# Audio tower on one core: another order of the token tiles, DCT tiles in three and two, and moved sums in the first gate

## The chip, the core and the metric

The kernel runs on one core of a Trainium2 chip. The metric is the device time of one execution in microseconds (us). A core has five engines that run their own instruction streams: TensorE (PE; PEld is its weight load), VectorE (DVE), ScalarE (ACT), GpSimd (POOL) and SyncE (SP), which here only issues transfers. Sixteen DMA engines move data between HBM and the core's memory. Matrix results land in PSUM.

## The reference, cut to what matters

The input is 64 rows of 80000 samples. Each row is cut into 157 frames of 512 samples; a frame is a token.

```
h = frames @ D.T                                   # orthonormal DCT of 512
y = layernorm(h)
key, query phases = tanh(y @ Wk), tanh(y @ Wq)     # 4 sets of 8 planes
V = y @ Wv
total = sum over sets of  weight * Re(cumsum(e^(i key) V) * conj(e^(i query)))
total = gate * total + (1 - gate) * positional part of the same form
h = h + y + (total / sqrt(8 * position)) @ Wo      # gate = sigmoid(y @ Wg)
z = layernorm(h)
expert = argmax(softmax(mean over tokens of z @ Wg2))     # 1 of 16, for each row
h = h + score * (z @ We[expert] + be[expert])
```

The cumulative sums are computed as causal attention: a matrix of scores between query and key tokens, masked so that a query sees keys up to its own position, and then a product with V.

## The kernel before, in words

**Groups and tiles.** Four rows of the input make a group (`GB` = 4), so there are 16 groups. The 157 tokens of a row are padded to 160 and cut into five blocks of 32 (`Q`). A token tile `n` holds block `n` of all four rows: 128 tokens. Tile 4 is `TAIL`. Within the transposed buffers (`xT`, `gT`) the tiles lie in the order of `SLOT`: slots 0 to 4 hold tiles 0, 1, TAIL, 2, 3.

**Scores.** `scores` (L596) multiplies, for each tile of 32 keys, the keys' phasors with those of a range of query slots, `SEES[n]`. A range has to be one stretch of slots that covers every query which may see the block. With tiles in order of position, tile 2 needs blocks 2, 3 and 4, and tile 3 needs 3 and 4; since TAIL lies in slot 2, both take slots 2 to 4. The widths are 160, 128, 96, 96 and 32 queries, `NS` = 512 in all. Where a range is wider than the causal one, `hmask` holds zeros. VectorE makes `att` from the scores: two versions of 512 columns (L597, L598).

**Read.** `read` (L611) works on one of four chunks of 128 features at a time. For each tile `n` and each of the four rows it multiplies the 32 keys' values (32 rows of the array, 128 columns of weights) with both versions of `att` in the tile's range. The four rows take four row groups of the array and run side by side, into four banks in two PSUM tiles. The first matmul of a bank has the start flag, so it has to cover all 320 columns. VectorE then multiplies the banks with the gate and adds (L619), four operations for each chunk.

**PSUM.** One pool of four tiles of two banks serves all stages, in rotation. An allocation waits until the tile four allocations back has been read for the last time.

**Order.** The order of the instructions is written out by hand. Each engine takes its instructions in that order, so a function that is called earlier stands earlier in all the queues that it uses. A period for group `g` is `project_and_values`, `gate`, `experts_and_embedding`, `attention`. In `experts_and_embedding` TensorE computes the five expert tiles of group `g - 1` (`expert`, L814, four column groups side by side) and the DCT of the five tiles of group `g + 1` (`embed`, L250 and L252, the whole array). `embed_statistics` is a ScalarE copy, four VectorE operations and four small POOL operations (L226 to L229, L265); `embed_res` is one ScalarE operation (L279), the last reader of the DCT tile's PSUM. `add_bv` adds a bias to two value tiles on POOL, `add_bias` and `expert_out` are VectorE operations on an expert tile, and `expert_out` issues its output transfers.

**Group 0** has no experts before it. `first_gate` interleaves its four gate parts (L558) with the DCT of group 1, with `weigh` (a VectorE scaling of the query phasors that the scores need), with `fold_twice(1, 1)` (four VectorE operations that prepare group 1's frames), with `add_bo` (a POOL addition) and with `weights`, which makes sums of weight quarters on VectorE, two of eight at a call.

**The end.** After the last group's attention the experts of group 14 run, five tiles in the order `ORDER` (TAIL, 0, 1, 2, 3). Within the second of them the last group's rows are routed, and `fetch` gathers its experts' weights with indirect transfers that POOL issues (L768), in two halves, with the expert bias (L798) between. The last group's experts follow: all tiles for the first half of the features, then tile by tile for the second. Outputs are issued by SP (L830), in the last group half of them by ScalarE.

Of the kernel before, what the change touches and what calls it, by code (L numbers as in the profile page):

```python
# [22 lines left out]
P = 128  # L23
# [9 lines left out]
HT = P // 2  # L33
HN = HT + 2 * P
LT = L - Q * TAIL
SETS, PLANES = 4, 8
F = SETS * PLANES
E = 16
# [2 lines left out]
ROUND = 1.5 * 2.0**23  # L41


SEES = [(0, LP), (Q, LP), (2 * Q, LP), (2 * Q, LP), (2 * Q, 3 * Q)]
START = [sum(hi - lo for lo, hi in SEES[:n]) for n in range(NM)]
NS = sum(hi - lo for lo, hi in SEES)

# [4 lines left out]
def audio_tower(ctx: ExitStack, tc: tile.TileContext, a, out):  # L52
# [69 lines left out]
    def fold_twice(g, m):  # L122

        if g < NG:
            ft, even = half(S[g]["xT"], m), S[g].pop(("even", m))
            add(ft[:, 2], even[:, 0], even[:, 1])
            sub(ft[:, 3], even[:, 0], even[:, 1])
            for n in range(2):
                to, by = ft[:, n], ft[:, 1 - n]
                nc.vector.scalar_tensor_tensor(to, by, lift[:, n : n + 1], to, ALU.mult, ALU.add)  # L130
# [416 lines left out]
    def weigh():  # L547
        nc.vector.tensor_scalar(qf[: 2 * F], qf[: 2 * F], wvec, None, ALU.mult)

    def gate_part(g, o):  # L550

        s = S[g]
        if o == 0:
            s["gT"] = p1.tile([P, C, 2 * HN], F32, tag="gT", name="gT")
        ps = psum()
        for k in range(2):
            for c in range(C):
                nc.tensor.matmul(  # L558
                    ps[:, k, :HN],
                    wg[:, c, o * P : (o + 1) * P],  # L560
                    half(s["xT"], k)[:, c],
                    start=(c == 0),
                    stop=(c == C - 1),
                )
        to = s["gT"][:, o].rearrange("p (m t) -> p m t", m=2)
        nc.scalar.activation(to, by_halves(ps), AF.Tanh, bias=hbg[:, o : o + 1], scale=0.5)
# [33 lines left out]
    def read(g, c):  # L600

        s = S[g]
        parts = [psum(), psum()]
        banks = [ps[:, b, : 2 * LP] for ps in parts for b in range(2)]
        for n in range(NM):
            for i in range(GB):
                q = slice(Q * i, Q * (i + 1))
                lo, hi = SEES[n]
                to = banks[i].rearrange("p (s t) -> p s t", s=2)[:, :, lo:hi]
                by = att[q, :, START[n] : START[n] + hi - lo]  # L610
                nc.tensor.matmul(  # L611
                    to, s["v", n][q, c * P : (c + 1) * P], by, start=(n == 0), stop=(n == TAIL)
                )
        for k, ps in enumerate(parts):
            of = slice(2 * k, 2 * k + 2)
            r = ps[:, :, : 2 * LP].rearrange("p b (s n t) -> p b s n t", s=2, n=NM)
            th = s["gT"][:, c].rearrange("p (n b t) -> p b n t", n=NM, b=GB)[:, of]
            for n, op in enumerate((ALU.mult, ALU.add)):
                nc.vector.tensor_tensor(th, r[:, :, n], th, op)  # L619
# [201 lines left out]

    def expert_out(g, n, ps):
        s = S[g]
        o = s["res"][n]
        nc.vector.scalar_tensor_tensor(o, ps, s["gate"], o, ALU.mult, ALU.add)  # L825
        for i in range(GB):

            for lo, hi in ((0, Q),) if n < TAIL else ((0, Q // 2), (Q // 2, LT)):
                queue = nc.sync if g + 1 < NG or i % 2 == 0 else nc.scalar
                queue.dma_start(out=out[GB * g + i, Q * n + lo : Q * n + hi, :], in_=o[Q * i + lo : Q * i + hi, :])  # L830

    def expert(g, n, between=lambda c: None):
        ps = psum()
# [84 lines left out]
    def first_gate():  # L918

        made = chain(weight_sums(wv, t_v), weight_sums(wo, t_o))  # L920

        def weights():
            next(made)
            next(made)

        gate_part(0, 0)
        embed(1, 1)
        embed_statistics(1, 1)
        weigh()
        embed_res(1, 1)  # L930
        fold_twice(1, 1)
        add_bo(0, 0)
        weights()
        gate_part(0, 1)
        scores(0)
        embed(1, 2)
        embed_statistics(1, 2)
        embed_res(1, 2)
        add_bo(0, 1)
        weights()  # L940
        gate_part(0, 2)
        for n in (3, TAIL):
            embed(1, n)
            embed_statistics(1, n)
        for n in (3, TAIL):
            embed_res(1, n)
        add_bo(0, 2)
        weights()
        gate_part(0, 3)
        for n in (3, TAIL):  # L950
            add_bo(0, n)
        weights()
        load_half(2, 0)
        load_half(2, 1)

# [61 lines left out]
    def experts_and_embedding(g):  # L1017

        new = g + 1

        def embedded(n):
            embed_statistics(new, n)
            embed_res(new, n)

        add_bias(g - 1, TAIL)
        expert(g - 1, TAIL)
        embed(new, 0)
        embed(new, 1)
        embed_statistics(new, 0)
        embed_statistics(new, 1)  # L1030
        add_bias(g - 1, 0)
        embed_res(new, 0)
        embed_res(new, 1)
        add_bv(g, 0)
        load_half(g + 2, 0)
        load_half(g + 2, 1)
        expert(g - 1, 0)
        embed(new, 2)
        embed_statistics(new, 2)
        embed_res(new, 2)  # L1040
        add_bias(g - 1, 1)
        add_bv(g, 1)
        expert(g - 1, 1)
        embed(new, 3)
        embed(new, TAIL)
        embed_statistics(new, 3)
        embed_statistics(new, TAIL)
        embed_res(new, 3)
        embed_res(new, TAIL)
        add_bias(g - 1, 2)  # L1050
        expert(g - 1, 2)
        add_bias(g - 1, 3)
        expert(g - 1, 3)
# [98 lines left out]
def _constants():  # L1152
    k = np.arange(D)[:, None].astype(np.float64)
    t = np.arange(D)[None, :].astype(np.float64)
    dct = np.cos(np.pi * (2.0 * t + 1.0) * k / (2.0 * D))
    scale = np.full((D, 1), np.sqrt(2.0 / D))
    scale[0, 0] = np.sqrt(1.0 / D)
    dct = (scale * dct).astype(np.float32)
    ahead = slice(0, P)

    angle = np.pi * (2.0 * np.arange(P)[:, None] + 1.0) / (2.0 * D)
    j = np.arange(P + 1)[None, :]
    cosines = np.sqrt(2.0 / D) * np.cos(angle) * np.where(j < P, np.cos(4 * j * angle), 0.0)
    sines = np.sqrt(2.0 / D) / np.cos(angle) * np.sin(4 * j * angle)

    tables = [cosines[:, :P].T, cosines[:, 1:].T, sines[:, :P].T, -sines[:, 1:].T, dct[0::4, ahead], dct[2::4, ahead]]

    def trig(half, n, turn):

        rows = np.array([[-1.0, -turn, PI / 2]] * half + [[1.0, turn, 0.0]] * half)  # L1170
        return np.tile(rows, (n, 1)).astype(np.float32)


    at = np.concatenate([np.arange(Q * n, Q * (n + 1)) for n in np.argsort(SLOT)])
    norm = 1.0 / np.sqrt(np.float64(PLANES) * (at + 1))
    causal = (np.arange(LP)[:, None] <= at[None, :]) * norm[None, :] * (at < L)[None, :]
    causal[L:] = 0.0
    masks = [causal[Q * n : Q * (n + 1), lo:hi] for n, (lo, hi) in enumerate(SEES)]
    setsel = np.tile(np.repeat(np.eye(SETS), PLANES, axis=0), (2, 1))
    f = lambda x: np.ascontiguousarray(x, dtype=np.float32)  # L1180

    sums = [x.sum(axis=0) for x in tables]
    table_sums = np.concatenate([sums[0] + sums[1], sums[2] + sums[3], sums[4], sums[5]]) / -D
    return {
        "dct_e": f(np.stack([dct[0::4, ahead].T, dct[2::4, ahead].T], axis=1)),
        "trig_o": f(np.stack([cosines, sines], axis=1)),
        "tables": f(np.stack(tables, axis=1)),
        "table_sums": f(table_sums),
        "lift": f(np.concatenate([np.tan(angle), -np.sin(angle) * np.cos(angle)], axis=1)),
        "ptrig": trig(PLANES, 1, 2 * PI),  # L1190
        "pos": f(np.tile(at, (2 * PLANES, 1))),
        "hmask": f(0.5 * np.tile(np.concatenate(masks, axis=1), (GB, 1))),
        "setsel": f(setsel),
        "revexp": f(np.tile(E - np.arange(E), (P, GB, 1))),
        "rowbase": f(np.stack([n * (np.arange(P) + P * E) + k for n, k in ((1, 0), (2, 0), (2, 1))], axis=1)),
    }
# [12 lines left out]
def _frames(x):  # L1209

    x = np.pad(x, [(0, 0), (0, LP * D - T_IN)]).reshape(NG, GB, NM, Q, C, P)
    x = np.stack([x[..., 0, :], x[..., 1, ::-1], x[..., 3, ::-1], x[..., 2, :]], axis=4)
    x = x[:, :, np.argsort(SLOT)].transpose(0, 5, 4, 2, 1, 3).reshape(NG, P, C, 2, HN)
    return np.ascontiguousarray(x.transpose(0, 3, 1, 2, 4))


# [34 lines left out]
```

## Time and profile before

| | |
|---|---|
| time, median of 3 | 1396.61 us (1396.16 to 1398.22) |
| profiled execution | 1396.78 us, span 1395.0 us |
| TensorE busy | 1383.8 us, 99% of the span |
| VectorE busy | 1033.5 us, 74% |
| GpSimd busy | 598.8 us, 43% |
| ScalarE busy | 399.7 us, 29% |
| moved by DMA | 119.72 MB, 86 GB/s on average |

The costliest lines on TensorE are the experts (L814, 270.3 us of busy time in the steady groups), the value and output products (L370), the gate products (L577) and the read (L611, 127.8 us). In the profile one fp32 matmul stands as two records, so that a tile of 16 expert matmuls is 32 records. Records of one tile on different row or column groups overlap, and a busy sum counts overlapping time once. The number behind `<-` in a waits line is the total in us, then how often, then the longest.

### The profile page before, as it was taken

Reading aid. Unit: us, or ns where it says so; the run is one execution under the profiler, and the core shown is the slowest. Engines: PE = TensorE matmul, PEld = TensorE weight load, DVE = VectorE, ACT = ScalarE, POOL = GpSimd, SP = SyncE. Lnnn points to the kernel's source line nnn. Section 1 sums busy time; section 2 is a strip of 40 time slices with the busy share of each in tenths; the row PEclk is TensorE's granted clock in tenths of the full one; section 3 lists DMA queues with packets and bytes.
Section 4 is the critical chain, followed back from the end, with each engine's and each line's share of the span. In section 5 each row is a group of like instructions: output and inputs, shape, how many; then the busy total and the mean of one; then the engine's idle time right before and its main releaser. Section 6 shows DMA issues by size and latency. Waiting matters only on the chain.

```text
span 1395.0 us, 26923 instructions
## 1 busy us (share of the span) xinstructions
PE 1383.8 (99%) x10656; PEld 919.3 (66%) x10656; DVE 1033.5 (74%) x2076; ACT 399.7 (29%) x690; POOL 598.8 (43%) x846
## 2 busy tenths in 40 slices
PE   9999999999999999999999999999999999999998
PEld 6677575766758667575675757667585675757762
DVE  5778686877868677786776868778686777867673
ACT  2414242231423314242141422314232142421410
POOL 2463544425543354534535444255533545345312
PEclk9999999999999999999999999999999999999999
DMA  7013204032230413205032140322304132040305
GB/s 223 1 39 128 76 28 162 16 130 75 86 116 3 153 53 129 76 1 184 21 129 76 40 152 14 133 73 106 97 2 147 59 128 76 1 151 16 129 8 195
DMA packets 47484, 119.72 MB, mean 86 GB/s; under 512 B 9264, under 2 KB 26176, under 8 KB 39424
## 3 DMA queue, kind: packets, MB, share of 16 engines
q0 software_dynamic: 11072, 71.31, 13.1%
q1 hardware_dynamic: 35788, 46.06, 11.3%
q8 instruction: 84, 1.38, 0.4%
q10 hardware_dynamic: 500, 0.64, 0.2%
q14 instruction: 40, 0.33, 0.1%
HBM read 97.41 MB, written 20.58 MB: 85 GB/s over the span
## 4 chain that ended last, share of the span: by engine, by line
PE 96%; DMA 1%; ACT 1%; DVE 1%; POOL 1%; issue 0%; SPq 0%; POOLq 0%; DVEq 0%; ACTq 0%
PE mm L370 27%; PE mm L814 20%; PE mm L577 16%; PE mm L611 9%; PE mm L235 9%; PE mm L250 3%; PE mm L687 3%; PE mm L522 3%; PE mm L252 2%; PE mm L596 1%; PE mm L296 1%; PE mm L196 1%; DMA t_v<-in_we,rows 1%; DMA wv<-in_wv 0%; PE mm L706 0%
## 5 line engine op out<-in xcount | busy, mean ns | idle before, releaser
L226 POOL TENSOR_SCALAR rstd<-mv 128x1 f32<-128x1 f32 x160 | 52.7, 329 | 522.3 <-DVE mv L224 514.8
L814 PE MATMUL mm<-we,x2T 128*32 128x512 f32 x2400 | 270.3, 595 | 0.0
L814 PEld LDWEIGHTS mm<-we,x2T 128*32 128x32 f32 x2400 | 71.8, 109 | 154.6 <-issue 144.6
L97 DVE TENSOR_TENSOR gT<-mm,gT 128x128 f32<-128x128 f32 (+1 forms) x135 | 87.0, 672 | 81.7 <-PE mm L577 80.2
L619 DVE TENSOR_TENSOR gT<-mm,gT 128x320 f32<-128x320 f32 x256 | 116.8, 487 | 28.7 <-PE mm L611 24.3
L611 PE MATMUL mm<-att,v 32*128 32x192 f32 (+2 forms) x2048 | 127.8, 371 | 0.7 <-ACT res_t L279 0.7
L611 PEld LDWEIGHTS mm<-att,v 32*128 32x128 f32 x2048 | 105.7, 185 | 21.8 <-issue 12.6
L587 ACT ACTIVATE gT<-gT,hbg 128x320 f32<-128x320 f32 x120 | 59.6, 554 | 169.3 <-DVE gT L97 169.3
L227 POOL TENSOR_TENSOR rstd<-rstd,power 128x1 f32<-128x1 f32 x160 | 98.2, 614 | 13.3
L674 ACT ACTIVATE x<-res,shift,rstd 128x512 f32<-128x512 f32 x64 | 52.1, 815 | 142.6 <-DVE res L97 109.5
L768 POOL DMA_INDIRECT we<-in_we,rows x60 | 62.1, 1034 | 71.4 <-DVE rows L764 57.6
L279 ACT ACTIVATE res<-mm,shift,rstd 128x512 f32<-128x512 f32 x64 | 49.8, 778 | 149.4 <-POOL rstd L265 118.3
L825 DVE SCALAR_TENSOR_TENSOR res<-mm,gate,res 128x512 f32<-128x512 f32 x64 | 48.0, 751 | 55.1 <-PE mm L814 55.0
L370 PE MATMUL mm<-t_o,sum 128*128 128x256 f32 x384 | 88.3, 379 | 0.4 <-DVE sum L96 0.4
L119 POOL TENSOR_TENSOR xT<-xT 128x640 f32<-128x640 f32 x30 | 46.8, 1559 | 91.6 <-DVE even L97 84.7
L97 DVE TENSOR_TENSOR v<-mm,v 128x512 f32<-128x512 f32 x105 | 70.7, 686 | 18.8 <-PE mm L370 18.4
L370 PE MATMUL mm<-t_v,sum 128*128 128x256 f32 x360 | 82.7, 379 | 0.0
L284 POOL TENSOR_TENSOR res<-res,bo 128x512 f32<-128x512 f32 x64 | 79.8, 1275 | 0.0
L370 PEld LDWEIGHTS mm<-t_o,sum 128*128 128x128 f32 x384 | 71.9, 190 | 11.7 <-PE mm L370 0.8
L97 DVE TENSOR_TENSOR res<-mm,res 128x512 f32<-128x512 f32 x96 | 65.2, 685 | 15.0 <-ACT u L630 11.8
L627 POOL TENSOR_TENSOR res<-res,u 128x512 f32<-128x512 f32 x45 | 56.1, 1273 | 42.1 <-DVE u L97 42.1
L235 PE MATMUL mm<-wv,xT 128*128 128x512 f32 x160 | 72.1, 593 | 0.0
(198 smaller groups left out, 2793.6 us busy)
## 6 DMA issues: line engine op xcount, KB each, us to landing
xT<-in_frames SPq DMA_DIRECT2D x32, 640.0 KB, 4.6
out<-res SPq DMA_DIRECT2D x248, 64.0 KB, 1.7
out<-res_t SPq DMA_DIRECT2D x62, 32.0 KB, 1.6
out<-res_t SPq DMA_DIRECT2D x62, 26.0 KB
wv<-in_wv SPq DMA_DIRECT2D x2, 512.0 KB, 5.6
wg<-in_wg SPq DMA_DIRECT2D x1, 1024.0 KB
wo<-in_wo SPq DMA_DIRECT2D x1, 1024.0 KB
we<-in_we,rows POOLq DMA_INDIRECT x60, 8.1
```

The source lines that it names most:

```text
L97: add = lambda *x: nc.vector.tensor_tensor(*x, ALU.add)
L227: nc.gpsimd.tensor_tensor(rstd, rstd, power, ALU.pow)
L235: nc.tensor.matmul(ps, tile_of(x[:, c], n), w[:, c, :], start=(c == 0), stop=(c == C - 1))
L284: nc.gpsimd.tensor_tensor(r, r, bo, ALU.add)
L370: nc.tensor.matmul(ps[:, b, :], lhs[:, c, P * b : P * (b + 1)], w[:, c, :], start=(c == 0), stop=(c == 1))
L577: nc.tensor.matmul(ps[:, o, :HN], w[:, c, o * P : (o + 1) * P], rhs[:, c], start=(c == 0), stop=(c == 1))
L587: nc.scalar.activation(to, to, AF.Tanh, bias=hbg[:, c : c + 1], scale=0.5)
L611: nc.tensor.matmul(to, s["v", n][q, c * P : (c + 1) * P], by, start=(n == 0), stop=(n == TAIL))
L619: nc.vector.tensor_tensor(th, r[:, :, n], th, op)
L627: more = lambda to, x: (nc.vector if last else nc.gpsimd).tensor_tensor(to, to, x, ALU.add)
L768: nc.gpsimd.indirect_dma_start(out=ws[b][:, n * k : n * (k + 1)], out_offset=None, in_=of, in_offset=bass.IndirectOffsetOnAxis(ap=rows[:, ...
L814: nc.tensor.matmul(ps[Q * i : Q * (i + 1), :], s["x2T"][:, c, i, Q * n : Q * (n + 1)], s["ws"][i][:, c, :], start=(c == 0), stop=(c == C - 1),
```

## The change

Five things change, and nothing of the arithmetic.

1. **Order of the token tiles.** A new list `BLOCK` = [1, 2, 3, 0, 4] says which block of positions tile `n` holds: tile 0 holds block 1, tile 3 holds block 0. The frames, the positions, the masks and the rows of the output follow it; the host arranges the frames. The slots now hold blocks 1, 2, 4, 3, 0, so that the queries of each key block are neighbours. `SEES` has the widths 128, 96, 64, 160 and 32, `NS` = 480.
2. **Order in `read`.** Tile 3, whose range covers all queries, comes first and has the start flag.
3. **DCT tiles in three and two.** In `experts_and_embedding` the DCT of tile 2, its statistics and its residual move in front of expert tile 0, next to those of tiles 0 and 1.
4. **First gate.** `weigh`, `fold_twice(1, 1)` and one pair of the weight sums move in front of the DCT of group 1's tile 1; a second pair moves in front of the DCT of tiles 3 and TAIL, and the other calls shift with them. `add_bo(0, 2)` joins those of tiles 3 and TAIL.
5. **Output queue.** In group 14 the output transfers of tiles 0, 1 and 2, twelve in all, are issued by POOL and not by SP.

```diff
+BLOCK = [1, 2, 3, 0, 4]
...
-SEES = [(0, LP), (Q, LP), (2 * Q, LP), (2 * Q, LP), (2 * Q, 3 * Q)]
+SEES = [(0, 4 * Q), (Q, 4 * Q), (2 * Q, 4 * Q), (0, LP), (2 * Q, 3 * Q)]
...
-        for n in range(NM):
+        for n in (3, 0, 1, 2, TAIL):
...
-                    to, s["v", n][q, c * P : (c + 1) * P], by, start=(n == 0), stop=(n == TAIL)
+                    to, s["v", n][q, c * P : (c + 1) * P], by, start=(n == 3), stop=(n == TAIL)
...
-        o = s["res"][n]
+        o, at = s["res"][n], Q * BLOCK[n]
...
+                if g + 2 == NG and n in ORDER[1:4]:
+                    queue = nc.gpsimd
-                queue.dma_start(out=out[GB * g + i, Q * n + lo : Q * n + hi, :], in_=o[Q * i + lo : Q * i + hi, :])
+                queue.dma_start(out=out[GB * g + i, at + lo : at + hi, :], in_=o[Q * i + lo : Q * i + hi, :])
...
         gate_part(0, 0)
+        weigh()
+        fold_twice(1, 1)
+        weights()
         embed(1, 1)
         embed_statistics(1, 1)
-        weigh()
         embed_res(1, 1)
-        fold_twice(1, 1)
         add_bo(0, 0)
         weights()
         gate_part(0, 1)
...
         gate_part(0, 2)
+        weights()
         for n in (3, TAIL):
             embed(1, n)
             embed_statistics(1, n)
         for n in (3, TAIL):
             embed_res(1, n)
-        add_bo(0, 2)
-        weights()
         gate_part(0, 3)
-        for n in (3, TAIL):
+        for n in (2, 3, TAIL):
             add_bo(0, n)
-        weights()
...
-        embed(new, 0)
-        embed(new, 1)
-        embed_statistics(new, 0)
-        embed_statistics(new, 1)
+        for n in range(3):
+            embed(new, n)
+            embed_statistics(new, n)
         add_bias(g - 1, 0)
-        embed_res(new, 0)
-        embed_res(new, 1)
+        for n in range(3):
+            embed_res(new, n)
...
         expert(g - 1, 0)
-        embed(new, 2)
-        embed_statistics(new, 2)
-        embed_res(new, 2)
...
-    at = np.concatenate([np.arange(Q * n, Q * (n + 1)) for n in np.argsort(SLOT)])
+    at = np.concatenate([np.arange(Q * BLOCK[n], Q * (BLOCK[n] + 1)) for n in np.argsort(SLOT)])
...
-    masks = [causal[Q * n : Q * (n + 1), lo:hi] for n, (lo, hi) in enumerate(SEES)]
+    masks = [causal[Q * BLOCK[n] : Q * (BLOCK[n] + 1), lo:hi] for n, (lo, hi) in enumerate(SEES)]
...
-    x = x[:, :, np.argsort(SLOT)].transpose(0, 5, 4, 2, 1, 3).reshape(NG, P, C, 2, HN)
+    x = x[:, :, np.array(BLOCK)[np.argsort(SLOT)]].transpose(0, 5, 4, 2, 1, 3).reshape(NG, P, C, 2, HN)
```

## The prediction

> **What bounds the kernel now.** I read the page first (busy shares, chain), then what TensorE waits for, then the timelines of the stages that the change touches.
>
> ```profile
> PE 1383.8 (99%) x10656; PEld 919.3 (66%) x10656; DVE 1033.5 (74%) x2076; ACT 399.7 (29%) x690; POOL 598.8 (43%) x846
> PE 96%; DMA 1%; ACT 1%; DVE 1%; POOL 1%; issue 0%; SPq 0%; POOLq 0%; DVEq 0%; ACTq 0%
> ```
>
> TensorE is the bound: 96% of the chain. Only fewer or shorter matmul slots, or the removal of one of its few waits, can pay. The waits of TensorE in full:
>
> ```profile
> PE mm L814 <- DMA spare<-in_we,rows: 1.4, 1, 1.4
> ...
> PE mm L558 <- ACT res L279: 1.2, 2, 0.8
> PE mm L814 <- DMA t_v<-in_we,rows: 0.8, 1, 0.8
> PE mm L611 <- ACT res_t L279: 0.7, 1, 0.7
> PE mm L596 <- POOL rstd L226: 0.6, 1, 0.6
> ```
>
> All of these lie in group 0 (60 to 78 us) or in the tail (after 1369 us); between them a period of 84.54 us repeats (reads begin at 500.04 and 584.57). A matmul record ends by a model, so I price work by the distance of starts. One period, experts with embedding, then the read:
>
> ```profile
> 561.80 3.64 PE L814 MATMUL mm<-we,x2T 128*32 128x512 f32 x32
> 565.37 0.71 PE L250 MATMUL mm<-dct_e,xT 128*128 128x128 f32 x4
> ...
> 567.36 3.64 PE L814 MATMUL mm<-we,x2T 128*32 128x512 f32 x32
> 570.93 0.71 PE L250 MATMUL mm<-dct_e,xT 128*128 128x128 f32 x4
> 571.47 0.61 PE L252 MATMUL mm<-trig_o,xT 128*128 128x129 f32 x4
> 572.01 3.64 PE L814 MATMUL mm<-we,x2T 128*32 128x512 f32 x32
> ...
> 577.57 7.07 PE L814 MATMUL mm<-we,x2T 128*32 128x512 f32 x64
> ```
>
> An expert tile takes 3.57 us when embedding follows, but two in a row take 7.00 (577.57 to 584.57), so an expert followed by an expert costs 3.43.
>
> ```profile
> 500.17 0.75 DVE L825 SCALAR_TENSOR_TENSOR res<-mm,gate,res 128x512 f32<-128x512 f32 x1 [2.02 <-PE mm L814]
> 502.14 3.79 DVE L619 TENSOR_TENSOR gT<-mm,gT 128x320 f32<-128x320 f32 x8 [1.22 <-PE mm L611]
> 506.19 3.79 DVE L619 TENSOR_TENSOR gT<-mm,gT 128x320 f32<-128x320 f32 x8 [0.26 <-PE mm L611]
> ```
>
> In the read VectorE takes 1.93 us for each of four chunks (3.79 us busy for two, next start included) while TensorE needs 1.84 (chunk starts 500.04, 501.93, 503.77): the two are nearly level, which decides how much a shorter read is worth.
>
> **What the Trainium skill says.** TensorE: Matmul & The Clock Gate, "LDWEIGHTS (loading the stationary operand)": a weight load takes columns/1.2 ns whatever the number of rows, so 107 ns for 128 columns. The trace agrees: a pass of the read's 64-wide matmul (54 ns of data) takes a slot of 112 ns, while 192, 256 and 320 wide take 162, 216 and 269. TensorEngine Tiling (Array Packing), "Key Properties": a change of the tiling mode drains TensorE. The trace shows a price for it, 0.14 us on the outgoing expert above and about 0.10 on the first and last embedding matmuls. DMA: Bandwidth & Descriptors, "Issuing engines are not separate DMA queues": transfers issued by any engine interleave on the same 16 engines. The tail agrees, see below.
>
> **The change, part by part.** Sums against the profiled span, 1395.0 us; the same execution ran 1396.78 and the median is 1396.61, so a difference is taken off the latter.
>
> *Read (L611).* Every fp32 matmul is two passes. Widths per chunk go from 320, 256, 192, 192, 64 to 320, 256, 192, 128, 64. By slots a 128-wide pass is max(108 of data, 112 of weight load) = 112, so two passes save 2 x (162 - 112) = 100 ns a chunk, 0.40 us a group, if TensorE alone decided. It does not. The third chunk needs PSUM that VectorE frees: its second half of row groups starts at 504.23, against 503.77 for the first, just after VectorE's first chunk ends (504.08), and this lag stays until 508.06, when the output product starts. Rebuilt: chunk 0 ends 0.10 earlier, so VectorE starts at 502.04 and ends two chunks at 505.83; the lagging half of the fourth chunk starts 0.145 later (the distance seen), at 505.97, and needs 1.97 - 0.10 = 1.87; the product starts at 507.85 instead of 508.06. Gain 0.21 us a group (bounds 0.10, VectorE alone, and 0.40, TensorE alone). The products after it find their data: VectorE is through at 509.8 and the last chunk is read only at 512.2. For 15 groups (0 is costed below): 3.2 us (1.5 to 6.0). That n = 3 now comes first costs nothing: its values and bias are ready some 6 us before (POOL ends at 578.6, the read starts at 584.6).
>
> *Scores (L596) and att.* Widths 160, 128, 96, 96, 32 become 128, 96, 64, 160, 32. The blocks of four tiles take 0.296, 0.218, 0.165 and, for 32 wide, still 0.175, so 64 wide stays at about 0.17: no gain (0 to 0.05 a group). The two VectorE operations lose 32 columns, off the path (they end long before the read). I take 0.
>
> *Embedding in three and two.* Embedding DCT tile 2 moves in front of expert tile 0. It removes one change to full tiles and back: before 3.57 + 1.98 + 3.57 + 1.09 + 3.57 + 1.98 + 7.00 = 22.77 us; after 3.57 + 2.87 + 7.00 + 1.98 + 7.00 = 22.44 (three tiles: 0.548, four inner blocks of 0.447, 0.541). Gain 0.33 us in 14 groups: 4.6 us. What moves with it: three DCT tiles hold three of the four PSUM buffers, so expert 1 takes the buffer of DCT tile 0 and starts at 571.69. VectorE's statistics of the third tile now stand ahead of the bias and the output of expert 0 (about 1.6 us later, needed only when expert 2 takes its buffer at 577.2). ScalarE copies the third sines before the first residual. POOL runs three rstd chains and then both bias additions, ahead of the chains of tiles 3 and 4; it frees at about 578, when the next chain is due. Tile 0's residual was done at 570.86, and its chain is untouched; slack 0.8 us. SP's order of loads and outputs is the same. Nothing waits by this.
>
> *Group 0's gate.* `weigh` no longer waits for the statistics of the next group's tile: the scores start 0.62 us earlier. But these statistics now stand behind fold_twice (1.9 us) and two weight sums (1.4) on VectorE, which can begin at 56.4, when the phasors end: so they run at 60.2 instead of 58.67. The residual at L279 ends near 64.5 instead of 63.43, and the gate part behind it, which waits for its PSUM, starts about 1 us later. What follows wins back: the sums of wo leave the place where they slowed POOL's chain (74.70 to 77.40, 2.7 us where 1.4 is usual), so the tail's residual ends near 77.6 instead of 78.22, and the second read chunk starts about 0.6 us earlier. With 0.1 to 0.2 from the narrower read I take 0.7 gained (-0.5 to 1.3).
>
> *Tail.* The last group's expert weights are gathered while the group before writes its output:
>
> ```profile
> 1363.77 0.94 POOL L768 DMA_INDIRECT spare<-in_we,rows  x1 [0.30 <-issue]
> 1365.01 0.94 POOL L768 DMA_INDIRECT t_v<-in_we,rows  x1 [0.30 <-issue]
> 1366.26 0.95 POOL L798 DMA_INDIRECT be<-in_be,expi  x1 [0.31 <-issue]
> ...
> 1371.24 0.94 POOL L768 DMA_INDIRECT t_v<-in_we,rows  x1 [0.30 <-issue]
> ```
>
> The first halves land at 1366.4, 1368.7, 1371.5 and 1373.3; TensorE, which could go on at 1369.9, starts its last 17.4 us at 1373.32. So 3.4 us are lost there, more than the 2.2 that the waits show. Of 3.0 MB moved up to 1373.3, about 0.6 MB are outputs. Twelve of these sixteen output transfers move to POOL's queue, behind all nine gathers. Then 2.4 MB at the same 293 KB/us would be in at 1371.2; at the 385 KB/us that a 4 KB packet of about 170 ns on 16 engines gives, at 1369.2. I take 1370.3: 3.0 us gained (2.1 to 3.4; below, 0). The second halves are needed 8.6 us after the start, 1378.9, and should be in by about 1377 (before: 1381.5, needed 1381.9). POOL then issues twelve outputs at 1.24 each, if they cost what a gather does (1.0 to 1.6): the last near 1387.1, landed by 1391.5 with the 4.4 us seen for outputs, in time for an end at 1392. Nothing of use is queued behind them.
>
> Sum: 3.2 + 0 + 4.6 + 0.7 + 3.0 = 11.5 us, so 1396.6 - 11.5 = 1385.1 us.
>
> **Rivals.**
> *Tail without gain* (20%): gathers are held by the rows they read rather than by outputs, or the twelve POOL issues cost 1.6 us or more and their landing (1372.2 + 19.2 + 4.4 = 1395.8) sets the end. Packets of 4 KB took 140 ns in the second half with outputs beside them, which speaks for the first. Gain 8.5: 1388.1.
> *Read bound by TensorE alone* (13%): VectorE's lag may not bind once the 64-wide slot is absorbed. Read 6.0 instead of 3.2: 1382.3. Against it: VectorE's 1.93 per chunk.
> *Part of the steady gain eaten* (9%): a group-0 wait of 1 to 2 us or a small wait in each period: gain 3 to 7, 1389.6 to 1393.6.
> *The other side* (4%): expert 1 waits for PSUM that DCT tile 0 holds. The price is 14 us for each us of wait; it decides against the change when tile 0's residual ends at 572.5 or later (slack 0.83, and 11.5/14 = 0.82 to cancel the gain). A POOL chain slowed as at 74.70 would end it at 572.2, a wait of 0.5: still a gain of 4.5. At a wait of 1.2 the time would be 1402.
>
> **How the numbers follow.** The sum as told has 54%: 1385.1, its own range 1383 to 1387. The range of 8 in 10 takes in the rival with a tail without gain and most of the TensorE-bound read: 1382.2 to 1389.5. What this kernel's times can tell from no change is 0.2%, 2.8 us. Faster: the sum, two first rivals and nearly all of the third, 0.95; same 0.015; slower 0.035.
>
> **What would show it.** The period falls from 84.54 to about 84.0: experts with embedding by 0.33, read start to output product from 8.02 to about 7.81. Read passes of 128 stand 112 ns apart. No wait of L814 on ScalarE's residual appears. In group 0 the wait of scores on POOL is gone and one on L279 grows to about 2 us. In the tail the last block starts 3 us sooner after the gathers' issue. Wrong would make it: an L814 wait in every period, or POOL's outputs landing last.

## The result and the profile after

The changed kernel takes 1387.74 us (median of 4 runs, 1385.92 to 1389.03) against 1397.01 for the kernel before (4 runs, 1396.16 to 1398.22). The ratio is 0.9932, with a 95% interval of 0.9915 to 0.9949: 9.3 us gained, between 7.1 and 11.9. The forecast was 1385.1, with a range of 1382.2 to 1389.5. The sign and the range held. Three of the five terms of the sum were off, and they are the instructive part.

The page of the profiled execution (1388.02 us, span 1386.3), its busy shares and the chain, and then what TensorE waits for (total in us, how often, the longest):

```profile
PE 1376.4 (99%) x10656; PEld 914.5 (66%) x10656; DVE 1030.7 (74%) x2076; ACT 402.9 (29%) x690; POOL 604.3 (44%) x858
PE 97%; DVE 1%; DMA 1%; ACT 1%; issue 0%; POOL 0%; SPq 0%; DVEq 0%; POOLq 0%
...
PE mm L560 <- ACT res L281: 2.9, 1, 2.9
...
PE mm L817 <- DMA t_v<-in_we,rows: 0.2, 1, 0.2
PE mm L817 <- DMA spare<-in_we,rows: 0.2, 1, 0.2
```

The bound is the same engine, and no new wait stands in the period: L817, the experts, does not wait for a residual anywhere, so the danger of the other side (expert 1 held by PSUM of DCT tile 0) did not come about. The waits for gathered weights went from 2.2 to 0.4 us. The one wait that grew is in group 0: L560, the gate part, waits once for 2.9 us, where it waited twice for 1.2 us together (L558 before). The waits of the scores (0.6) and of the read (0.7) there are gone.

One period of the timeline of TensorE (start, duration, what):

```profile
560.35 3.64 PE L817 MATMUL mm<-we,x2T 128*32 128x512 f32 x32
563.92 0.71 PE L252 MATMUL mm<-dct_e,xT 128*128 128x128 f32 x4
...
566.79 7.07 PE L817 MATMUL mm<-we,x2T 128*32 128x512 f32 x64
573.80 0.71 PE L252 MATMUL mm<-dct_e,xT 128*128 128x128 f32 x4
...
575.78 7.07 PE L817 MATMUL mm<-we,x2T 128*32 128x512 f32 x64
582.78 1.80 PE L614 MATMUL mm<-att,v 32*128 32x320 f32 x32
```

Start to start: 3.57 + 2.87 + 7.01 + 1.98 + 7.00 = 22.43 us from the first expert tile to the read. The forecast's sum had 22.44 (its terms as printed add up to 22.42), and before it took 22.77. Reads begin at 498.83 and 582.78: the period is 83.95, against 84.54.

The span fell from 1395.0 to 1386.3, by 8.7 us. Cut at the starts of the first and the last read (before 75.15 and 1322.63, after 78.72 and 1315.86), it divides as follows:

| stretch | before | after | difference |
|---|---|---|---|
| span's start to the first read | 75.15 | 78.72 | +3.57 |
| first read to the last | 1247.48 | 1237.14 | -10.34 |
| last read to the end | 72.37 | 70.44 | -1.93 |

The first row is partly paid back at once: the first read itself waited before (9.85 us long) and doesn't now (7.82). The output product of group 0 starts at 86.54 instead of 85.00, so the first gate costs 1.54 us in this execution, where 0.7 gained had been forecast. These 2.03 us of the first read are part of the middle row; the other 8.31 are the steady gain, 14 periods of 0.59, where read and embedding had been forecast at 0.54 together. The last row is less than its forecast of 3.0 and the read's 0.2.

### The profile page after: what moved, and what is told of

Its sections match the earlier page's. It is cut to its first block, busy times and chain, and to the rows that moved or that the text cites. A ratio compares the mean times of both kernels' runs of the same rounds, so it can differ in the third digit from the quotient of the medians.

```text
span 1386.3 us, 26936 instructions
## 1 busy us (share of the span) xinstructions
PE 1376.4 (99%) x10656; PEld 914.5 (66%) x10656; DVE 1030.7 (74%) x2076; ACT 402.9 (29%) x690; POOL 604.3 (44%) x858
## 4 chain that ended last, share of the span: by engine, by line
PE 97%; DVE 1%; DMA 1%; ACT 1%; issue 0%; POOL 0%; SPq 0%; DVEq 0%; POOLq 0%
PE mm L372 27%; PE mm L817 20%; PE mm L579 17%; PE mm L614 9%; PE mm L237 9%; PE mm L252 3%; PE mm L690 3%; PE mm L524 3%; PE mm L254 2%; PE mm L598 1%; PE mm L298 1%; PE mm L198 1%; PE mm L560 1%; DMA t_v<-in_we,rows 0%; DMA wv<-in_wv 0%; PE mm L709 0%
## 5 line engine op out<-in xcount | busy, mean ns | idle before, releaser
L228 POOL TENSOR_SCALAR rstd<-mv 128x1 f32<-128x1 f32 x160 | 44.6, 279 | 515.8 <-DVE mv L226 505.9
L817 PE MATMUL mm<-we,x2T 128*32 128x512 f32 x2400 | 267.4, 594 | 0.0
L817 PEld LDWEIGHTS mm<-we,x2T 128*32 128x32 f32 x2400 | 73.2, 110 | 161.3 <-issue 157.1
L614 PE MATMUL mm<-att,v 32*128 32x256 f32 (+3 forms) x2048 | 123.6, 359 | 0.0
L286 POOL TENSOR_TENSOR res<-res,bo 128x512 f32<-128x512 f32 x64 | 85.6, 1366 | 0.0
L231 POOL TENSOR_SCALAR shift<-mv,rstd 128x1 f32<-128x1 f32 x160 | 70.7, 442 | 16.5
```

The source lines that it names most:

```text
L231: nc.gpsimd.tensor_scalar(shift, mv[:, 0:1], rstd, -1.0, ALU.mult, ALU.mult)
L286: nc.gpsimd.tensor_tensor(r, r, bo, ALU.add)
L614: nc.tensor.matmul(to, s["v", n][q, c * P : (c + 1) * P], by, start=(n == 3), stop=(n == TAIL))
L817: nc.tensor.matmul(ps[Q * i : Q * (i + 1), :], s["x2T"][:, c, i, Q * n : Q * (n + 1)], s["ws"][i][:, c, :], start=(c == 0), stop=(c == C - 1),
```

## The experiments

My theory after seeing this was that the steady part works as the sum says, that the gate's new wait takes back what was won there, and that the gathers of the tail are limited by more than the outputs beside them. The rivals for each are in the expectations.

### One part at a time

Four kernels make one part of the change each, starting from the kernel before. They share a chip and its runs of the kernel before (median 1397.42).

**The order of the token tiles alone** (`BLOCK`, `SEES`, the order in `read`, and what follows from them):

```diff
-SEES = [(0, LP), (Q, LP), (2 * Q, LP), (2 * Q, LP), (2 * Q, 3 * Q)]
+SEES = [(0, 4 * Q), (Q, 4 * Q), (2 * Q, 4 * Q), (0, LP), (2 * Q, 3 * Q)]
...
-        for n in range(NM):
+        for n in (3, 0, 1, 2, TAIL):
```

> The kernel before with the new order of the token tiles and of the read alone. My theory (VectorE's lag binds): read start to output product 7.82 us instead of 8.02 in every group, period 84.54 - 0.20 = 84.34, group 0 about 0.2 shorter, tail unchanged; time 3.2 us under before. Rival (TensorE alone decides the read): 7.62 us, period 84.14, 6.4 us under before.

Measured: 1393.14 us (7 runs, 1392.68 to 1393.93), ratio 0.9971 (0.9959 to 0.9982), 4.3 us gained. In its profile the read takes 7.82 us instead of 8.02 and the period 84.28 instead of 84.54. The read's 0.20 was forecast; the other 0.06 was not. It is in the scores: 40 matmuls that took 1.02 us from first start to the next product take 0.965. From the start of one pass (four matmuls side by side) to the start of the next it is 0.056 us at 64 columns and 0.083 at 96, and each tile has two passes. I had read "no gain" from the 32-wide block at the end of the stage, whose 0.175 us is mostly the way to the next product and not a floor of the matmul.

**The DCT tiles in three and two alone:**

```diff
-        embed(new, 0)
-        embed(new, 1)
-        embed_statistics(new, 0)
-        embed_statistics(new, 1)
+        for n in range(3):
+            embed(new, n)
+            embed_statistics(new, n)
...
-        embed(new, 2)
-        embed_statistics(new, 2)
-        embed_res(new, 2)
```

> The kernel before with the DCT tiles in three and two alone. My theory (one change between column tiles and the full array is saved, nothing waits): period 84.54 - 0.33 = 84.21 in groups 1 to 14, read still 8.02; 4.6 us under before. Rival (the third PSUM tile makes an expert wait): an L814 wait on ScalarE's residual in every period and a period above 84.3.

Measured: 1392.84 us (1392.49 to 1393.14), ratio 0.9969 (0.9957 to 0.9980), 4.6 us gained, with a period of 84.20 (0.34 less) and a read of 8.02. The period's 0.34 is the term's 0.33 as well as can be read; the timed 4.6 has an interval of 2.8 to 6.0.

**The first gate alone:**

```diff
         gate_part(0, 0)
+        weigh()
+        fold_twice(1, 1)
+        weights()
         embed(1, 1)
         embed_statistics(1, 1)
-        weigh()
         embed_res(1, 1)
-        fold_twice(1, 1)
...
```

> The kernel before with the new first gate alone. Theory of a clock drop behind the wait: the gate part after the second DCT tile waits about 2.9 us for the residual, TensorE's granted clock then falls to a half for 6 to 7 us, the gate part takes about 7.2 us instead of 4.5, and the output product of group 0 starts near 86.7 instead of 85.0: 1.7 us slower. Rival (the slow clock of the changed kernel was chance and has nothing to do with the wait): the same wait of 2.9 us, but a gate part of 4.5 us at full clock, the output product near 83.9: 1.1 us faster than before.

Measured: 1397.63 us (12 runs, 1396.39 to 1399.49), ratio 1.0002 (0.9993 to 1.0011). Nothing is gained on average, and the runs are spread over 3.1 us. Its profiled execution was one of the quickest (1396.43): there the product of group 0 starts at 84.09, 0.9 earlier than before, close to the 0.7 that the forecast had. In this execution the numbers of the expectation's rival came out, and not the slow gate part. So the wait of 2.8 us alone doesn't explain why the median shows no gain.

**The output queue alone** (twelve outputs of group 14 on POOL's queue):

```diff
+                if g + 2 == NG and n in ORDER[1:4]:
+                    queue = nc.gpsimd
```

> The kernel before with twelve output transfers of group 14 issued by POOL alone. Theory (the gathers of the first halves were slowed by outputs, but are limited by their own packets once these are gone): first half of the last gather lands 6.5 us after its issue instead of 8.3, the last block of experts starts 1.8 us sooner; 1.8 us under before. Rival (outputs were the whole of it, as predicted): 3.0 us. All periods stay 84.54.

Measured: 1396.62 us (12 runs, 1396.36 to 1397.16), ratio 0.9996 (0.9987 to 1.0005). That is 0.8 us gained, with an interval from 1.8 gained to 0.7 lost, where 3.0 had been forecast and 1.8 expected. In its profile the last block of experts starts 49.84 us after the start of the last read, against 50.69 before.

The four add up to -4.3 - 4.6 + 0.2 - 0.8 = -9.5, and the whole change was measured at -9.3. The parts don't interfere with each other by anything these runs can see.

### The first gate: a wait and a clock

In the profile after, the gate part behind the long wait lasts 7.38 us for 16 records, where the same part took 4.57 in the kernel before. First the line of before, then the lines of after:

```profile
63.48 4.57 PE L558 MATMUL mm<-xT,wg 128*128 128x320 f32 x16 [0.40 <-ACT res L279]
```

```profile
60.25 1.03 PE L598 MATMUL mm<-qf,kf 128*32 128x128 f32 x40
61.22 0.71 PE L252 MATMUL mm<-dct_e,xT 128*128 128x128 f32 x4
61.77 0.61 PE L254 MATMUL mm<-trig_o,xT 128*128 128x129 f32 x4
65.32 7.38 PE L560 MATMUL mm<-xT,wg 128*128 128x320 f32 x16 [2.94 <-ACT res L281]
```

Its busy time by windows (us, busy us and records of TensorE, the share of its full clock that TensorE was granted, share of DMA, GB/s):

```profile
60.00:64.00 4.00, 2.38 (x50) 1.00 0.00 0
64.00:66.00 2.00, 0.68 (x1) 0.55 0.00 0
66.00:68.00 2.00, 2.00 (x5) 0.50 0.00 0
68.00:70.00 2.00, 2.00 (x5) 0.50 0.00 0
70.00:72.00 2.00, 2.00 (x7) 0.75 0.00 0
72.00:75.00 3.00, 3.00 (x22) 1.00 0.03 5
```

While TensorE waits, its clock falls to half, at 64.19, and it returns at 71.02, 6.83 us later. Of these TensorE works from 65.32 on, 5.70 us at half speed, so 2.85 are lost, and 7.38 - 4.57 = 2.81 is what the gate part is longer than it was before. The page's row of the clock shows nothing of it: a slice there is 35 us long. It takes narrow windows, or a duration that doubles, to see it.

In the profile of the first gate alone the same part stands behind a wait of nearly the same length, at full clock:

```profile
64.90 4.57 PE L558 MATMUL mm<-xT,wg 128*128 128x320 f32 x16 [2.76 <-ACT res L279]
```

The Trainium skill has a reason why this can differ from one execution to the next: TensorE: Matmul & The Clock Gate, "Part 1: The HAM clock gate (the "warmup" mystery)", says that the clock is halved after an idle window of about 3.4 us and restored after a busy one, and that the windows of 3413 ns run freely, not aligned to the kernel. The traces agree on the length: the clock was low for 6.83 us in the kernel after, in both of its profiled executions, and for 3.41 in two more kernels with the same wait that are told of below; two windows and one. On what sets it off they differ: a wait of 2.9 us was enough, in four of five profiled executions that had such a wait, and the fall came when TensorE had been idle for 1.8 us (after), 2.3 (its repeat), 2.7 and 2.9 us. In the fifth, the gate alone, the clock falls at the end of the run, at 1394.16; counted back from there in steps of 3413 ns, an edge between two windows lay at about 63.0, 0.9 us into the wait. This is an estimate with that page's figure, and that the place of the edge decided it is not shown. Three kernels test whether the long wait is the cause; they and a repeat of the kernel after ran on one chip (kernel before: 1397.48).

The kernel after again:

> The changed kernel once more, for a comparison on one chip. Theory (a chance clock drop behind the long wait in group 0): about 9.5 us under before, with a spread of the single times of up to 3 us, against about 1 us in the kernels without that wait. Rival (the drop belongs to the kernel whatever the wait): every time alike.

Measured: 1389.17 us (1387.64 to 1391.59, 5 runs), ratio 0.9941 (0.9927 to 0.9954). Again the runs are spread, by 4 us, and the profile has the wait of 2.94 and a clock at half from 64.38 to 71.21. The product of group 0 starts at 86.50.

Twelve matmuls that nobody uses, put into the wait (`scores` hands out its PSUM tile for them):

```diff
...
-        scores(0)
+        both = scores(0)
         embed(1, 2)
+        for _ in range(12):
+            nc.tensor.matmul(both[:, 1, :P], ident, ident, start=True, stop=True)
...
```

> The changed kernel with twelve matmuls more, which nothing uses, put on TensorE in the place of its wait of 2.9 us in group 0. Theory (idle time of TensorE is what lets the clock fall): no stretch at half clock, the gate part behind takes 4.5 us at most, read of group 0 starts near 75.5, single times within 1 us of each other, median 1 to 2 us under the changed kernel although work was added. Rival (the drop is chance and not tied to idle time): same spread of 3 us and the same median.

Measured: 1388.51 us (1387.47 to 1388.97), ratio 0.9933 (0.9919 to 0.9946). That is 0.7 us under the repeat of the kernel after, where 1 to 2 had been expected, and the two intervals overlap. Some idle time is left, since the first of the added matmuls (L946) waits for VectorE's reading of the tile of PSUM that they share with the scores; from then on they last until the gate part begins, at 66.28, about 1 us after its residual is ready:

```profile
PE mm L946 <- DVE att L600: 1.2, 1, 1.2
```

The clock stays full, and the product starts at 84.60, 1.9 earlier than in the repeat, though these matmuls compute nothing.

The first gate in its order of before, all else as after:

```diff
         gate_part(0, 0)
-        weigh()
-        fold_twice(1, 1)
-        weights()
         embed(1, 1)
         embed_statistics(1, 1)
+        weigh()
         embed_res(1, 1)
+        fold_twice(1, 1)
...
```

> The changed kernel with the first gate of before. Theory: waits of 0.4 to 0.8 us in group 0, no clock drop; the output product of group 0 starts at 84.8 (85.0 less 0.2 of the read); about 9.5 us under before with a spread of 1 us: the new gate gives nothing on average. Rival (the new gate is a gain of 0.7 us in itself, as predicted): 0.7 us slower than the changed kernel.

Measured: 1388.83 us (1388.59 to 1390.66), ratio 0.9940 (0.9926 to 0.9953), the same as the kernel after within what these runs can tell. Full clock, product at 84.81.

A third order, that takes the early scores without the long wait. `weigh` and `fold_twice` stay in front, but the sums of weights no longer stand beside the statistics and the small POOL operations that the next gate part hangs on:

```diff
         weigh()
         fold_twice(1, 1)
-        weights()
         embed(1, 1)
         embed_statistics(1, 1)
         embed_res(1, 1)
-        add_bo(0, 0)
-        weights()
         gate_part(0, 1)
         scores(0)
+        add_bo(0, 0)
+        weights()
...
```

> The changed kernel with a first gate in a third order: weigh and fold_twice early, the statistics of group 1's tile 1 next on VectorE, then the scores, and the weight sums behind both. Theory (what made the wait is the two sums ahead of these statistics and the two that run beside POOL's small operations): the wait behind the second DCT tile falls from 2.9 to about 0.8 us, no clock drop, no wait ahead of the last gate part, the output product of group 0 starts near 82.3; about 13 us under before. Rival (the long wait comes from POOL's chain itself): a wait of over 2 us stays.

Measured: 1387.08 us (1386.38 to 1387.46), ratio 0.9924 (0.9911 to 0.9938): 10.4 us under the kernel before and 2.1 under the kernel after on this chip. Its five runs all lie under every run of the other three there, and their spread is the narrowest of the four. Its waits of L560, which were one of 2.9:

```profile
PE mm L560 <- ACT res L281: 1.3, 2, 0.8
```

The first and the last of the four POOL operations that the gate part hangs on, in the kernel after and then in this one:

```profile
61.95 0.48 POOL L228 TENSOR_SCALAR rstd<-mv 128x1 f32<-128x1 f32 x1 [7.46 <-DVE mv L226]
64.24 0.22 POOL L267 TENSOR_SCALAR rstd<-rstd 128x1 f32<-128x1 f32 x1
```

```profile
60.40 0.21 POOL L228 TENSOR_SCALAR rstd<-mv 128x1 f32<-128x1 f32 x1 [6.11 <-DVE mv L226]
61.59 0.22 POOL L267 TENSOR_SCALAR rstd<-rstd 128x1 f32<-128x1 f32 x1
```

With the sums beside them they take 2.51 us, without them 1.41. The product of group 0 starts at 83.23. I had expected about 82.3, no wait ahead of the last gate part and 13 us under the kernel before; but a wait of 0.80 is left there, behind a chain on POOL that takes 2.50 us (66.47 to 68.97) and has sums of weights beside it again (VectorE, from 66.30 on).

Every profiled execution with idle times of 1.3 us or less there kept its clock, and four of five with 2.8 to 2.9 lost it. The filled kernel keeps all else and lost nothing, in its profile and by the mean clock of 1.000 in all five of its runs.

How often the clock fell in the runs without a profile can be read from the mean granted clock, which is on record for every run of the experiments and of the kernel after. In the profiles with full clock in the gate this mean is 0.999 or 1.000, in those with half clock 0.997 to 0.999; so 0.998 or less marks a fall. Such a mean stands beside 8 of the 21 runs of the kernels that have the long wait and were repeated (2 of 4 and 2 of 5 of the kernel after, 4 of 12 of the gate alone), in none of the 41 of the six other kernels that were repeated, and in none of 39 of the kernel before. For the gate alone it divides the times:

| mean granted clock | runs | us |
|---|---|---|
| 1.000 | 5 | 1396.39 to 1397.20, median 1396.72 |
| 0.999 (either is possible) | 3 | 1397.40 to 1398.16 |
| 0.997 and 0.998 | 4 | 1397.86 to 1399.49, median 1398.55 |

Against the 1397.42 of the kernel before, the new gate gains 0.7 us at full clock, which is the forecast, and loses 1.1 where the clock fell (medians of five and of four runs). Its median of no gain is a mixture of the two. The one run of the kernel after with a mean of 1.000 took 1385.92 us, 0.8 above the forecast time.

### The read: whose time it is

The forecast made the read 0.21 us shorter where TensorE alone would have given 0.40, on the ground that VectorE's work on each chunk (1.93 us) holds up the third and fourth. Leaving out the second of VectorE's two operations on each pair of banks takes that lag away; the sum is then incomplete, and only the timing counts.

```diff
-            for n, op in enumerate((ALU.mult, ALU.add)):
+            for n, op in enumerate((ALU.mult,)):
```

With the read of before:

> The kernel before, whose read leaves out the second of VectorE's two operations on each pair of banks (the addition of the other half to the product with the gate), so the output differs. This halves VectorE's work in the read: about 0.97 us a chunk against 1.93, far below TensorE's 1.84. Theory (VectorE's lag sets the second half of chunks 2 and 3): the lag goes, and the time from the start of the read to the output product falls from 8.02 to four chunks of TensorE alone, about 7.4 to 7.6. Rival (TensorE alone sets the read, and the narrower matmuls gained only half of their slots for another reason): it stays at 8.02.

And with the read of after:

> The kernel after with the same addition in the read left out, so the output differs. Theory: the read falls from 7.82 to about 7.0 to 7.2, so that the difference to the kernel before with the same cut is 0.40 us, the 4 x 100 ns of slots that TensorE alone would gain. Rival: the difference stays at 0.20.

The starts of the chunks on TensorE, and of the product that follows, with the read of before and then of after (the second from its second chunk on):

```profile
498.43 1.90 PE L611 MATMUL mm<-att,v 32*128 32x320 f32 x32
500.32 1.85 PE L611 MATMUL mm<-att,v 32*128 32x320 f32 x32
502.17 1.85 PE L611 MATMUL mm<-att,v 32*128 32x320 f32 x32
504.01 1.85 PE L611 MATMUL mm<-att,v 32*128 32x320 f32 x32
505.96 1.99 PE L370 MATMUL mm<-wo,gT 128*128 128x256 f32 x8
```

```profile
495.77 1.75 PE L614 MATMUL mm<-att,v 32*128 32x320 f32 x32
497.51 1.75 PE L614 MATMUL mm<-att,v 32*128 32x320 f32 x32
499.25 1.75 PE L614 MATMUL mm<-att,v 32*128 32x320 f32 x32
501.10 1.99 PE L372 MATMUL mm<-wo,gT 128*128 128x256 f32 x8
```

From the read's start to the product it is 505.96 - 498.43 = 7.53 us, and 7.12 with the narrower matmuls: 0.41 apart, 1.74 a chunk against 1.84, just the 0.10 that the slots gave. With VectorE's full work it was 8.02 and 7.82. So TensorE won 0.41 us a group, and 0.21 of it went straight into a longer wait for VectorE, whose lag now costs 7.82 - 7.12 = 0.70 where it cost 0.49. The whole kernel with the read of after and the cut took 1375.47 us in one run, that with the read of before 1389.50 (the kernel before: 1396.83 on this chip). The lag is plain in the timeline of VectorE in the kernel after:

```profile
500.84 3.79 DVE L622 TENSOR_TENSOR gT<-mm,gT 128x320 f32<-128x320 f32 x8 [1.11 <-PE mm L614]
504.78 3.79 DVE L622 TENSOR_TENSOR gT<-mm,gT 128x320 f32<-128x320 f32 x8 [0.15 <-PE mm L614]
```

Between the second chunk and the third it idles for only 0.15 us (0.26 before): it is the pace of the read now.

### The tail: what holds the gathers

With the outputs moved away, the first halves of the last weights were in sooner, by less than forecast. Issues on POOL in the kernel after, and when TensorE starts its last block, and last that start in the kernel before:

```profile
1354.18 1.07 POOL L771 DMA_INDIRECT wv<-in_we,rows  x1 [8.29 <-DVE logit L783]
...
1358.04 0.94 POOL L771 DMA_INDIRECT t_v<-in_we,rows  x1 [0.31 <-issue]
...
1365.21 2.07 POOL L835 DMA_DIRECT2D out<-res  x4
1367.74 0.50 POOL L835 DMA_DIRECT2D out<-res  x1 [0.46 <-DVE res L811]
...
1364.57 0.62 PE L817 MATMUL mm<-t_v,x2T_last 128*32 128x512 f32 x1 [0.21 <-DMA t_v<-in_we,rows]
```

```profile
1373.32 0.62 PE L814 MATMUL mm<-t_v,x2T_last 128*32 128x512 f32 x1 [0.78 <-DMA t_v<-in_we,rows]
```

The first half of `t_v` was issued at 1358.04 and is there at 1364.5, 6.5 us later; before, it was 8.3 (1365.01 to 1373.3). From the start of the last read to that block it is 48.71 us, against 50.69 before. Of these 1.98 the shorter read has 0.21, so the queue gave 1.8 in this execution. The trace shows nothing else moving while these gathers wait: between 1356 and 1362 only what POOL's gathers read is carried, and yet at 208 to 276 KB (of 1024 bytes) in each us. I had counted on 293 at the least. To see whether the few outputs left matter, one kernel leaves out all output transfers of group 14:

```diff
             for lo, hi in ((0, Q),) if n < TAIL else ((0, Q // 2), (Q // 2, LT)):
+                if g + 2 == NG:
+                    continue
```

> The kernel after with the output transfers of group 14 left out, so part of the output is not written. Theory (the gathers of the last expert weights are held by themselves once the outputs are behind them): the last block still starts 48.7 us after the start of read 15, within 0.3, and the first gathers still move some 220 to 280 KB/us. Rival (what is left of output traffic holds them): the last block starts 1 us or more earlier. If TensorE stalls labelled issue stand in the last expert tiles here too, about 46 us after the start of read 15, then the issue of output transfers is not their cause.

Measured, in one run: 1387.04 us. Reads and gathers are as above, and the last block starts at

```profile
1363.57 0.62 PE L817 MATMUL mm<-t_v,x2T_last 128*32 128x512 f32 x1 [0.20 <-DMA t_v<-in_we,rows]
```

The last read began at 1314.25, so this is 49.3 us after it: not earlier than in the kernel after but 0.6 later, outside the 0.3 that I allowed. The first six us carry 176 to 312 KB each. The rival had it 1 us or more earlier, so it falls as far as one run can tell: once the outputs stand behind the gathers, no gain is left in leaving them out. What sets this rate I did not find. (This kernel is one of the two others in which the clock was at half once more, from 64.84 to 68.26; the kernel after with the cut read is the other.)

A second thing hides part of the queue's gain. In the profiles of all kernels on the two chips of the one-part and gate runs, TensorE stops in the last expert tiles, mostly in steps of 0.4 to 0.8 us, for nothing that the trace can name:

```profile
PE mm L814 <- issue: 1.6, 3, 0.8
```

This is the kernel with the three-and-two tiles alone. In six of the eight kernels the first such stop ends 47 us after the last read's start, before any wait for a gather; in the read alone and the gate alone it ends 50.3 and 50.6 us after. The kernel with the queue alone has 0.7 us of them; from the start of its last read to its end it takes 72.1 us, and the three other one-part kernels 72.8 to 73.0, which agrees with the timed 0.8. In the repeat of the kernel after, with 1.6 us of stops, the last block starts 51.28 us after the last read, where it was 48.71 in the first profile and 50.69 before: nothing is left there of the queue's 1.8. The stops are absent from the profiles of before and after shown above and from the three kernels that leave work out, which ran on a third chip. I did not find their cause, nor whether outputs bring them about.

## Why the prediction was right, and where it was not

| term of the sum | forecast, us gained | what the runs showed |
|---|---|---|
| read | 3.2 (0.21 a group) | 0.20 a group |
| scores | 0 | 0.055 a group, 0.9 in all |
| embedding | 4.6 (0.33 a group) | 0.34 a group, 4.6 timed |
| first gate | 0.7 | -0.2 timed (interval -1.5 to 1.0): 0.7 at full clock, -1.1 where the clock fell; -1.5 in the profile of the kernel after |
| tail | 3.0 | 0.8 timed, 1.8 in the first profile of the kernel after, none in its repeat |
| sum | 11.5 | 9.3 (7.1 to 11.9) |

*Read: right, and for the stated reason.* VectorE's lag was the whole difference between 0.21 and 0.40; the two kernels with the cut show TensorE alone at 0.41. The rival of a read bound by TensorE alone falls.

*Embedding: right.* The sum of starts gave 22.44 and the trace 22.43. No wait for PSUM appeared.

*Scores: mis-sized.* I priced 64 columns by the 32-wide block, which ends its stage. The right price was in the differences between blocks in the middle.

*First gate: the step that failed.* It said that the gate part would start about 1 us later, and that the earlier scores and the moved sums would win this back. The wait was longer: the residual ended at 65.27 instead of near 64.5. POOL's chain for it took 2.5 us (61.95 to 64.46) beside the sums of weights that were moved to just that place (VectorE, 61.71 to 62.97). I had seen this very slowing in the profile before, at 74.70, booked its end as a gain, and not asked where the sums would slow the next chain. And a wait was priced as its length alone. At full clock this still came out as forecast (0.7 gained in the five runs of the gate alone with a mean clock of 1.000, 0.9 in its profile); with the clock at half the part cost 2.8 more in the profile of the kernel after. The forecast put that at nothing.

*Tail: mis-sized.* The rate of the gathers without outputs beside them was taken as 293 to 385 KB/us; it is 208 to 276 in the first six full us. So the rival of a tail without gain was nearer than the chosen 3.0, by the timed 0.8 and by its total of 1388.1 too, though the first profile's 1.8 lies between the two. That the gathers are held by the rows they read, as it said, is not shown; only that leaving out the outputs does not free them. The 140 ns that it gave for packets of 4 KB with outputs beside them are not in the trace of before either, where they take 159 ns (median, 1373 to 1381). POOL's outputs were feared at 1.0 to 1.6 us each; they cost 0.50, the last is issued at 1375.2, eleven us before the end, and TensorE waits for none of them.

The forecast time missed by 2.6 us. Of this 0.4 is the kernel before, which ran at 1397.0 here and 1396.6 there. The other 2.2 are, by the timed runs, 2.2 too much in the tail and 0.9 in the gate, against 1.1 too little in the read and its scores together; this leaves 2.0, and the intervals are wider than the rest. That the total fell well inside its range owes something to luck: the gate and the tail gave less than forecast, the scores more, and these partly cancelled.

## What to carry to other kernels

Price a step from the starts of its neighbours, and where two engines are nearly level, rebuild the stage with both of them: half of what one of them gains may go into waiting for the other. Long waits of TensorE have a second price beyond their length, so an order with waits of 0.5 and 0.8 us can beat one with a single wait of 2.9, and a spread of 3 to 4 us between runs of a kernel whose traces differ only there is a hint to look at the granted clock, in narrow windows and run by run. When work that slows another engine is moved, look at what it will stand beside in its new place.

## What the runs showed that I had not expected

- The TensorE clock at half for 3.41 or 6.83 us in and after a wait of 2.94 us, from 1.8 us of idle time on, in some executions and not in others, at a cost of 1.6 to 3.0 us.
- With the same wait, the mean granted clock of each run (0.998 or less against 1.000) told the longer runs from the shorter: medians of 1398.55 and 1396.72 us for the gate alone.
- Four small POOL operations took 2.51 us with VectorE's sums of weights beside them and 1.41 without.
- Gathers of 4 KB packets, alone on the DMA engines, at 208 to 276 KB/us over their first six full us, and 340 to 384 KB/us later (1362 to 1365).
- A direct output transfer issued by POOL occupies it for 0.50 us, an indirect one for 0.94 with 0.30 between two.
- A 64-wide pass of the scores at 0.056 us where a 96-wide one takes 0.083.
- Stops of TensorE of 0.4 to 0.8 us in the last expert tiles, in all eight profiles on two chips and in none of the other five, whose cause is open.
